# Sums for the first output projection formed inside the loop, in the memory of the finished chunks

## The chip, the cores and the metric

The kernel runs on one core of one Trainium2 chip. The metric is the device time of one execution in microseconds (us). TensorE is called PE, VectorE DVE, ScalarE ACT, GpSimd POOL, and SyncE (which only issues transfers here) SP.

## The reference

Two layers work on `x` of shape (2, 512, 32, 32) in fp32. Layer 0 is attention with sampled keys: for each of 2 images and 8 groups, 64 sample positions are predicted, keys and values are gathered there, and a small network (2 to 128 to 128 to 1) turns every pair of a query position (1024) and a sample position (64) into a bias. After the softmax, the part that matters here follows:

```
out = einsum('bhij,bhjd->bhid', attn, vh)           # heads
out = einsum('bchw,oc->bohw', out, out_w) + out_b   # first output projection
x = x + out
h1 = gelu(einsum('bchw,oc->bohw', bn(x), mlp_w1) + mlp_b1)
x = x + einsum('bchw,oc->bohw', h1, mlp_w2) + mlp_b2
```

Layer 1 is a single-head attention over the 1024 positions of each image with residual.

## The kernel before, in words

**Loop.** Most of the time is a loop of 256 iterations, `for s in range(NS)`, 16 for each of 16 groups (an image `b`, a pair of heads `k`, a half `f`). An iteration evaluates the bias network for four sample positions: `st_layer1` (line 548, DVE) writes `h1` (128x4096), two iterations ahead, in three buffers; `st_layer2` (line 565, PE) multiplies it in 64 recorded matmuls; ACT moves the results out of PSUM into `rx`, `ua`, `ub` (lines 571 and 573); `st_sum` (line 581, DVE) adds them in pairs; POOL issues a transfer that adds `ub` into `ua` (line 583); `st_layer3` (line 604, PE) reduces pairs of iterations into logits, once in two iterations. Beside the loop run two generators, a step per iteration: `bg`, which samples keys and values for the later groups in five chains (`chain`, `sample`), and `tail`, which is the softmax of the group before (`softmax_steps`) and writes the attention weights over the queries in `qa[:, b, k, :]`. The values, already multiplied with the output weights, lie in `vp`.

**First output projection.** After the loop, `project(b, ...)` multiplies `vp` by `qa` for each image as a 2x2 block product in seven products in place of eight. In the order of the code the products are 1, 2, 5, 6, 7, 3, 4; they are called p1, p2, p5, p6, p7, p3, p4 below, and p1' to p4' for image 1. Each is 8 recorded matmuls of 128x512 at line 796. The method needs sums of blocks first: `fold` forms three sums of weight blocks and overwrites a fourth (four adds of 128x512, line 714, on POOL), `spread` does the same for the blocks of `qa` (four adds of 128x1024, lines 717, 718, 719 and 721, on DVE). p1 and p2 read only untouched blocks; p5, p6, p3 and p4 read sums. Image 0 has its sums in a tile `op0`, image 1 in `op1` and `op2`.

**What stands on DVE and PE after the loop.** Each product leaves PE in one of three PSUM buffers of the pool `zp`, and DVE empties it into `xs` or into a temporary (lines 730 and 804), so a product can only start when the one three places before it has been emptied. The softmax of the last group is still to be done then: PE turns its logits (`pt`, line 629), DVE takes the maximum (lines 636 and 637), ACT does the exponentials (642), DVE the reciprocal (647), ACT the scaling (651), PE turns the result back (`pb`, line 660), ACT copies it into `qa` (663), and image 1's `spread` needs it. These steps are queued on DVE among the sums and the emptying of products. The order on each engine is made by a scheduler at build time; each engine then works its own list in order.

**Loads.** SP loads `xs` in sixteen transfers once the loop's buffers below it are free, then the weights of the following MLP in units (`load_unit`: a `w1t` and a `w2t` tile, each with a `fold` on POOL). The MLP's matmuls are at line 850.

Of the kernel before, what the change touches and what calls it, by code (L numbers as in the profile page):

```python
# [8 lines left out]
F32 = mybir.dt.float32  # L9
AF = mybir.ActivationFunctionType  # L10
ALU = mybir.AluOpType
# [3 lines left out]
P = 128  # L15
B, C, H, W = 2, 512, 32, 32
HW = H * W
NCH = C // P
# [8 lines left out]
CHAINS = [[(0, 0)], [(0, 1)], [(0, 2), (0, 3)], [(1, 0), (1, 1)], [(1, 2), (1, 3)]]  # L27
# [21 lines left out]
def conv_seq_kernel(ctx: ExitStack, tc: tile.TileContext, x, xt, kst, cst, vec, wsm, outw, w1, w2, wl, out):  # L49
    nc = tc.nc  # L50
# [28 lines left out]
    qa = cp.tile([P, B, NCH, HW], F32, tag="big", name="qa")  # L79
# [4 lines left out]
    vp = f_pool.tile([P, NCH * B, C], F32, tag="vp", name="vp")  # L84
    sx = f_pool.tile([P, 8, 2, J], F32, tag="sx", name="sx")

    zpp, simpp = (tc.tile_pool(name=n, bufs=c, space=PSUM) for n, c in (("zp", 3), ("simp", 2)))
    zp, simp = zpp.__enter__(), simpp.__enter__()

# [1 line left out]
        return zp.tile([P, 2, 512], F32, tag="ps2", name=name).rearrange("p h n -> p (h n)")  # L91

    groups = [(b, k, f) for b in range(B) for k in range(NCH) for f in range(2)]
    with tc.tile_pool(name="lp", bufs=2) as lp, tc.tile_pool(name="ph", bufs=1) as ph:


        def wake(src, n):
# [575 lines left out]
        for s in range(NS):  # L673
            if s > 0:
                st_sum(s - 1, 2)
            if s % 4 == 0 and s // 4 + 1 < 4 * NG:
                load_tables(s // 4 + 1)
            if s + 2 < NS:
                st_layer1(s + 2)
            st_layer2(s)  # L680


            if s % 4 == 0 and s // 4 + 1 < 4 * NG:
                with tc.issue_after(evicted[s][0]):
                    st_tables(s // 4 + 1)
            st_sum(s, 0)
            with tc.issue_after(evicted[s][1]):
                next(bg, None)
            if tail is not None:
                with tc.issue_after(evicted[s][s % 4 == 0]):  # L690
                    tail = tail if next(tail, 0) is None else None
            if s % 2 == 1 and s >= 3:
                st_layer3(s - 3)
                if (s - 2) % NSL == NSL - 1:
                    tail = softmax_steps(s // NSL - 1)
# [1 line left out]
        st_layer3(NS - 2)  # L697
        tail = softmax_steps(NG - 1)
        next(tail)

    PARTS = {1: (0, 0), 2: (1, 2), 3: (6, 3), 4: (2, 6), 5: (4, 4), 6: (5, 5), 7: (3, 1)}  # L710

    def fold(engine, w, sign=ALU.add):
        for o, u, v, op in ((4, 3, 2, sign), (5, 4, 0, ALU.add), (6, 5, 1, sign), (3, 3, 0, ALU.add)):
            engine.tensor_tensor(w[o], w[u], w[v], op)  # L714

    def spread(x, last=True):
        nc.vector.tensor_tensor(x[4], x[0], x[1], ALU.subtract)
        nc.vector.scalar_tensor_tensor(x[5], x[4], -1.0, x[3], ALU.mult, ALU.subtract)
        nc.vector.tensor_tensor(x[1], x[3], x[1], ALU.subtract)
        if last:  # L720
            nc.vector.scalar_tensor_tensor(x[6], x[5], -1.0, x[2], ALU.mult, ALU.subtract)

    def multiply(pool, order, product, took):
        for p in order:
            ps = pool.tile([P, 2, 512], F32, tag="ps2", name="sw")
            product(ps, *PARTS[p])
            took[p](ps)

    def plus(out, a, b_, op=ALU.add):
        nc.vector.tensor_tensor(out, a, b_, op)  # L730


    def load_g(g, i):
# [25 lines left out]
        nc.vector.scalar_tensor_tensor(t4, t2, -1.0, q[2], ALU.mult, ALU.subtract)  # L759
        return [q[0], t3, q[2], q[3], t1, t2, t4]  # L760

    with tc.tile_pool(name="mp", bufs=1) as mp:
        halves = [(b, h) for b in range(B) for h in range(2)]
        units = [(b, p) for b in range(B) for p in range(NU)]
        wts, accs = {}, {}
# [1 line left out]
        def load_unit(b, p):  # L767
            ws_ = []
            for i, w in enumerate((w1, w2)):
                wt = mp.tile([P, 7, 2, 256], F32, tag=f"w{i + 1}t", name=f"w{i + 1}t", bufs=2)  # L770
                nc.sync.dma_start(out=wt[:, 0:4], in_=w[:, p])
                fold(nc.gpsimd, [wt[:, j] for j in range(7)])
                ws_.append(wt)
            wts[b, p] = ws_
# [6 lines left out]
                load_unit(*units[0])  # L781


        def project(b, parts, wsum, between=lambda: None):
            v, q = vp[:, b * NCH : b * NCH + NCH, :], qa[:, b]
            w = [v[:, k : k + 2, n : n + 256] for k, n in ((0, 0), (2, 0), (2, 256), (0, 256))]
            w += [wsum[:, j] for j in range(3)]
            fold(nc.gpsimd, w)
            x = [q[:, k : k + 2, n : n + 512] for k in (0, 2) for n in (0, 512)] + [parts[:, j] for j in range(3)]
            x11, x12, x21, x22 = quarters(b)  # L790
            t = parts[:, 3]

            def go(ps, a, b_):
                for m in range(2):
                    for k in range(2):
                        nc.tensor.matmul(  # L796
                            ps[:, m, :], w[a][:, k, m * P : (m + 1) * P], x[b_][:, k, :],
                            start=(k == 0), stop=(k == 1),
                        )


            def first(dst, o, u, op):
                for m in range(2):
                    nc.vector.scalar_tensor_tensor(
                        dst[:, m, :], dst[:, m, :], col("outb", o + m), u[:, m, :], ALU.add, op
                    )

            def o1(ps):
                nc.scalar.copy(t, ps)
                first(x11, 0, ps, ALU.add)  # L810

            def o5(ps):
                plus(x22, x22, ps, ALU.subtract)
                plus(x12, x12, ps)

            def o6(ps):
                plus(t, t, ps)
                first(x12, 0, t, ALU.add)

            def o7(ps):  # L820
                plus(t, t, ps)
                first(x22, 2, t, ALU.subtract)
                first(x21, 2, t, ALU.subtract)

            spread(x)
            took = {
                1: o1, 2: lambda ps: plus(x11, x11, ps), 5: o5, 6: o6, 7: o7,
                3: lambda ps: plus(x12, x12, ps), 4: lambda ps: plus(x21, x21, ps, ALU.subtract),
            }
            for p in (1, 2, 5, 6, 7, 3, 4):  # L830
                multiply(zp, (p,), go, took)
                between()


        def normalise(b):
            xb = mp.tile([P, 7, 2, 512], F32, tag="xb", name="xb")
            for j, (o2, h) in enumerate(((0, 0), (0, 1), (1, 0), (1, 1))):
                for m in range(2):
                    o = 2 * o2 + m
                    nc.scalar.activation(  # L840
                        xb[:, j, m, :], xs[:, o, b, h * 512 : (h + 1) * 512], AF.Identity,
                        bias=col("bn2b", o), scale=bns[:, 4 + o : 5 + o],
                    )
            return xb

        def product(w, x):
            def go(ps, a, b_):
                for m in range(2):
                    for k in range(2):
                        nc.tensor.matmul(  # L850
                            ps[:, m, :], w[:, a, k, m * P : (m + 1) * P], x[:, b_, k, :],
                            start=(k == 0), stop=(k == 1),
                        )
            return go
# [34 lines left out]
        def layer2(b, p, w, hm):  # L889
# [31 lines left out]
            plus(v[3], v[3], p5, ALU.subtract)  # L921


        op0 = mp.tile([P, 7, 2, 512], F32, tag="xb", name="op0")
        project(0, op0, op0[:, 4:6].rearrange("p a k n -> p (a k n)")[:, 0:1536].rearrange(
            "p (a k n) -> p a k n", k=2, n=256
        ), lambda: [next(tail, None) for _ in range(3)])
        for _ in tail:
            pass
        xb = normalise(0)  # L930
        op1 = mp.tile([P, 4, 2, 512], F32, tag="acc", name="op1")
        project(1, op1, mp.tile([P, 3, 2, 256], F32, tag="w2t", name="op2", bufs=2))
        spread([xb[:, j] for j in range(7)])
        load_unit(*units[1])
        for pl in (simpp, zpp):
# [22 lines left out]
    with tc.tile_pool(name="sp", bufs=1) as sp:  # L958
# [3 lines left out]
        for b in range(B):  # L962
# [75 lines left out]
            def turn(u, e):  # L1038
                for i in range(2):
                    for m in range(2):  # L1040
                        ps = mq.tile([P, 2, 512], F32, tag="ps2", name="psx")
                        for c in range(8):
                            nc.tensor.transpose(
                                ps[:, c // 4, c % 4 * P : (c % 4 + 1) * P], e[i][:, m, c * P : (c + 1) * P], ident
                            )
                        n = 256 * u + m * P
                        nc.scalar.copy(  # L1047
                            aT[:, i : i + 3 : 2, :, n : n + P],
                            ps.rearrange("p a (c n) -> p a c n", n=P),
                        )  # L1050
                n = slice(256 * u, 256 * u + 256)
                spread([aT[:, j, :, n] for j in range(6)], last=False)

            e0 = scores(0)
            e1 = scores(1)
# [184 lines left out]
```

## Time and profile before

| | us |
|---|---|
| median of 4 runs (2739.53 to 2742.7) | 2741.31 |
| profiled execution, its own time | 2742.95 |
| span of the profile of that execution | 2741.2 |
| PE busy | 2718.9 (99%) |
| DVE busy | 2246.9 (82%) |
| ACT busy | 1686.7 (62%) |
| POOL busy | 374.1 (14%) |
| end of the last loop matmul group, start of p1 | 1988.6 |
| start of the first MLP matmul (line 850) | 2048.36 |

Times in the text are from the start of the span. The profile gives, for each engine, its instructions in order of time, and in brackets how long the engine stood idle before one and what released it. An entry with a count merges several instructions; matmul ends are modelled, so the distance between starts is the better measure on PE.

### The profile page before, as it was taken

Reading aid. Unit: us, or ns where it says so; the run is one execution under the profiler, and the core shown is the slowest. Engines: PE = TensorE matmul, PEld = TensorE weight load, DVE = VectorE, ACT = ScalarE, POOL = GpSimd, SP = SyncE. Lnnn points to the kernel's source line nnn. Section 1 sums busy time; section 2 is a strip of 40 time slices with the busy share of each in tenths; the row PEclk is TensorE's granted clock in tenths of the full one; section 3 lists DMA queues with packets and bytes.
Section 4 is the critical chain, followed back from the end, with each engine's and each line's share of the span. In section 5 each row is a group of like instructions: output and inputs, shape, how many; then the busy total and the mean of one; then the engine's idle time right before and its main releaser. Section 6 shows DMA issues by size and latency. Waiting matters only on the chain.

```text
span 2741.2 us, 46612 instructions
## 1 busy us (share of the span) xinstructions
PE 2718.9 (99%) x20114; PEld 993.8 (36%) x20114; DVE 2246.9 (82%) x1327; ACT 1686.7 (62%) x2164; POOL 374.1 (14%) x430
## 2 busy tenths in 40 slices
PE   9999999999999999999999999999999999999999
PEld 3322323233434323333333333333344444446455
DVE  6999999998999999999999999999774574466454
ACT  4786897788878788876866776686622022124040
POOL 3111111111111111111111111111162232000000
PEclk9999999999999999999999999999999999999999
DMA  5444444444444444444444444444331011000000
GB/s 184 93 95 91 93 99 86 94 101 95 84 91 99 98 85 85 97 90 86 91 94 86 85 95 89 88 93 86 70 138 44 34 46 46 16 16 0 31 0 31
DMA packets 64685, 214.32 MB, mean 78 GB/s; under 512 B 11104, under 2 KB 13664, under 8 KB 61792
## 3 DMA queue, kind: packets, MB, share of 16 engines
q0 software_dynamic: 36864, 135.28, 26.7%
q1 hardware_dynamic: 26752, 74.98, 7.8%
q8 instruction: 159, 2.61, 0.4%
q10 hardware_dynamic: 864, 1.07, 0.1%
q14 instruction: 46, 0.38, 0.0%
HBM read 71.59 MB, written 6.55 MB: 29 GB/s over the span
## 4 chain that ended last, share of the span: by engine, by line
PE 95%; ACT 2%; DVE 1%; issue 1%; DMA 1%; SPq 0%; DVEq 0%; ACTq 0%
PE ps L565 62%; PE sw L850 14%; PE sw L967 9%; PE sim L604 4%; PE sw L1065 2%; PE sw L796 1%; PE psg L454 1%; PE sim L595 1%; DMA fb<-fdr 0%; ACT rx L571 0%; PE pkv L380 0%; PE pt L629 0%; PE pb L660 0%; ACT prod L245 0%; DVE acc L237 0%
## 5 line engine op out<-in xcount | busy, mean ns | idle before, releaser
L565 PE MATMUL ps<-h,cw 128*32 128x512 f32 x16384 | 1789.6, 592 | 7.9 <-ACT rx L571 4.9
L548 DVE CUSTOM_DVE_ANT_1 h<-ta,tb 128x4096 f32<-128x4096 f32 (+1 forms) x257 | 1131.7, 4404 | 87.1 <-PE ps L565 83.4
L565 PEld LDWEIGHTS ps<-h,cw 128*32 128x32 f32 x16384 | 553.2, 110 | 1205.4 <-issue 1149.1
L571 ACT ACTIVATE rx<-ps,sc 128x1024 f32<-128x1024 f32 x512 | 568.9, 1111 | 219.3 <-PE ps L565 215.1
L583 POOL DMA_DIRECT2D ua<-ub x254 | 220.4, 868 | 1696.1 <-DVE ub L581 1608.2
L573 ACT ACTIVATE ua<-ps,sc 128x1024 f32<-128x1024 f32 x256 | 308.4, 1205 | 117.0 <-PE ps L565 116.8
L573 ACT ACTIVATE ub<-ps,sc 128x1024 f32<-128x1024 f32 x256 | 308.0, 1203 | 88.5 <-PE ps L565 88.2
L581 DVE SCALAR_TENSOR_TENSOR ua<-rx,sc,ua 128x1024 f32<-128x1024 f32 x256 | 327.3, 1278 | 34.7 <-ACT ua L573 34.7
L581 DVE SCALAR_TENSOR_TENSOR ub<-rx,sc,ub 128x1024 f32<-128x1024 f32 x256 | 326.6, 1276 | 5.8 <-ACT ub L573 5.6
L850 PE MATMUL sw<-xb,w1t 128*128 128x512 f32 x448 | 193.7, 592 | 1.3 <-DVE xs L730 1.3
L850 PE MATMUL sw<-hm,w2t 128*128 128x512 f32 x448 | 193.6, 592 | 0.0
L730 DVE TENSOR_TENSOR hm<-hm,sw 128x1024 f32<-128x1024 f32 x56 | 67.6, 1220 | 112.5 <-PE sw L850 112.3
L604 PE MATMUL sim<-ua,w3s 128*32 128x512 f32 x1024 | 135.4, 594 | 0.0
L850 PEld LDWEIGHTS sw<-xb,w1t 128*128 128x128 f32 x448 | 85.0, 190 | 108.8 <-issue 105.7
L850 PEld LDWEIGHTS sw<-hm,w2t 128*128 128x128 f32 x448 | 85.1, 190 | 107.1 <-issue 106.4
L859 ACT ACTIVATE hm<-hm,vs 128x512 f32<-128x512 f32 x64 | 42.7, 714 | 129.5 <-DVE hm L730 129.5
L730 DVE TENSOR_TENSOR xs<-xs,sw 128x1024 f32<-128x1024 f32 (+1 forms) x48 | 55.5, 1170 | 75.7 <-PE sw L967 36.0
L529 ACT ACTIVATE ta<-fb,vs 128x512 f32<-128x512 f32 x64 | 88.6, 1384 | 18.2 <-DMA fb<-fdr 18.2
L967 PE MATMUL sw<-aT,vt 128*128 128x512 f32 x224 | 96.7, 593 | 0.3 <-ACT aT L1047 0.3
L884 ACT COPY hm<-sw 128x1024 f32<-128x1024 f32 x8 | 8.1, 1009 | 133.5 <-PE sw L850 133.5
L714 POOL TENSOR_TENSOR w1t<-w1t 128x512 f32<-128x512 f32 x32 | 59.8, 1887 | 112.0 <-DMA w1t<-in_w 111.3
L245 ACT ACTIVATE prod<-qa,vs 128x56 f32<-128x56 f32 (+4 forms) x180 | 64.2, 440 | 0.0
(221 smaller groups left out, 1551.1 us busy)
## 6 DMA issues: line engine op xcount, KB each, us to landing
ua<-ub POOLq DMA_DIRECT2D x254, 512.0 KB, 4.7
fb<-fdr SPq DMA_DIRECT2D x64, 512.0 KB, 5.2
w1t<-in_w SPq DMA_DIRECT2D x8, 1024.0 KB, 5.0
w2t<-in_w SPq DMA_DIRECT2D x8, 1024.0 KB, 5.0
xn<-in_x SPq DMA_DIRECT2D x8, 512.0 KB, 5.3
xnt<-in_xt SPq DMA_DIRECT2D x8, 512.0 KB, 5.9
xs<-in_x SPq DMA_DIRECT2D x16, 256.0 KB, 6.1
out<-xs SPq DMA_DIRECT2D x16, 256.0 KB, 2.1
```

What stands on the lines that cost most here:

```text
L245: nc.scalar.activation(dst, src, AF.Copy, scale=col("dww", 12 * m + t))
L529: nc.scalar.activation(ta.rearrange("p j x -> p x j"), fb[:, 0], AF.Identity, bias=col("cb1"), scale=col("w1x"))
L548: nc.vector._custom_dve(TENSOR_ADD_SAT, out=h1[:, y : y + step].rearrange("p y t x -> p (y t x)"), in0=a.unsqueeze(1).to_broadcast([P, ste ...
L565: nc.tensor.matmul(ps[32 * q : 32 * q + 32, h, :], cw2[:, 32 * z : 32 * z + 32], h1[:, 16 * h : 16 * h + 16, q, :], start=True, stop=True,)
L571: nc.scalar.activation(o, ps, AF.Relu, bias=sc[:, 4 + z : 5 + z])
L573: nc.scalar.activation(o, ps, AF.Relu, bias=sc[:, 4 + z : 5 + z], scale=sc[:, z : z + 1])
L581: nc.vector.scalar_tensor_tensor(r[1], r[0], sc[:, z : z + 1], r[1], ALU.mult, ALU.add)
L583: nc.gpsimd.dma_start(out=sums[s][1], in_=sums[s][3], accum_op=ALU.add)
L604: nc.tensor.matmul(sims[gi][q : q + 32, :], w3s[:, 28 - 4 * i : 60 - 4 * i], sums[s + e][z][:, h, :], start=(i == 0), stop=(i == NSL // 2 ...
L730: nc.vector.tensor_tensor(out, a, b_, op)
L850: nc.tensor.matmul(ps[:, m, :], w[:, a, k, m * P : (m + 1) * P], x[:, b_, k, :], start=(k == 0), stop=(k == 1),)
L967: nc.tensor.matmul(ps[:, m, :], w[:, a, k, c + m * P : c + (m + 1) * P], x[b_][:, k, :], start=(k == 0), stop=(k == nk - 1),)
```

## The change

The temporaries of the chains (pool `ph`) are put at the other end of the memory (`side="right"`). As soon as the last chain has ended, inside the loop, that pool is closed and a pool `op` is opened in its place, with tiles for image 0's sums. The eight adds of image 0's projection are issued from the loop, one per four iterations in the code, and all on DVE. `project` no longer forms sums; image 1's come from `fold` on POOL and `spread` on DVE after the loop, as before, but into buffers that are otherwise the second `w1t` and `w2t`. The MLP's activations get a pool opened after the projection of image 0. In the built program, DVE's list has the eight adds within iterations' work that is about 100 iterations ahead of the loop's end; the order of the two loads of the second MLP unit is reversed, and both stand behind the projection of image 1.

```diff
-    with tc.tile_pool(name="lp", bufs=2) as lp, tc.tile_pool(name="ph", bufs=1) as ph:
+    php = tc.tile_pool(name="ph", bufs=1, side="right")
+    ph = php.__enter__()
+    with tc.tile_pool(name="lp", bufs=2) as lp:
...
+            if bg is not None and state.get(len(CHAINS) - 1, 0) is None:
+                bg = None
+                php.__exit__(None, None, None)
+                opp = tc.tile_pool(name="op", bufs=1, side="right")
+                op = opp.__enter__()
+                op0 = op_blocks(
+                    0, op.tile([P, 3, 2, 512], F32, name="op0x"), op.tile([P, 3, 2, 256], F32, name="op0w")
+                )
+                opt = op.tile([P, 2, 512], F32, name="opt")
+                ready = s
+            if bg is None and s > ready and (s - ready) % 4 == 0 and (s - ready) // 4 <= 8:
+                i = (s - ready) // 4 - 1
+                if i < 4:
+                    spread(op0[1], (i,))
+                else:
+                    fold(nc.vector, op0[0], which=(i - 4,))
...
-                wt = mp.tile([P, 7, 2, 256], F32, tag=f"w{i + 1}t", name=f"w{i + 1}t", bufs=2)
+                wt = wp.tile([P, 7, 2, 256], F32, name=f"w{i + 1}t")
...
-        def project(b, parts, wsum, between=lambda: None):
+        def project(b, w, x, t, between=lambda: None):
-            fold(nc.gpsimd, w)
-            spread(x)
...
-        op0 = mp.tile([P, 7, 2, 512], F32, tag="xb", name="op0")
-        project(0, op0, ...)
+        op1w = wp.tile([P, 5, 2, 256], F32, tag="w2t", name="op1w")
+        op1 = op_blocks(1, wp.tile([P, 3, 2, 512], F32, tag="w1t", name="op1x"), op1w)
+        fold(nc.gpsimd, op1[0])
+        project(0, op0[0], op0[1], opt, lambda: [next(tail, None) for _ in range(3)])
         for _ in tail:
             pass
+        opp.__exit__(None, None, None)
+        mp = top.enter_context(tc.tile_pool(name="mp", bufs=1, side="right"))
         xb = normalise(0)
-        op1 = mp.tile([P, 4, 2, 512], F32, tag="acc", name="op1")
-        project(1, op1, mp.tile([P, 3, 2, 256], F32, tag="w2t", name="op2", bufs=2))
+        spread(op1[1])
+        project(1, *op1, op1w[:, 3:5].rearrange("p a k n -> p a (k n)"))
```

The new function `op_blocks(b, parts, wsum)` only names the blocks: four views of `vp` and three of `wsum`, four views of `qa` and three of `parts`. `fold` and `spread` now take a list of which of their four adds to issue.

## The prediction

> **What bounds the kernel now.** First the page: busy time by engine, and the chain that ended last by engine.
>
> ```profile
> PE 2718.9 (99%) x20114; PEld 993.8 (36%) x20114; DVE 2246.9 (82%) x1327; ACT 1686.7 (62%) x2164; POOL 374.1 (14%) x430
> ...
> PE 95%; ACT 2%; DVE 1%; issue 1%; DMA 1%; SPq 0%; DVEq 0%; ACTq 0%
> ```
>
> PE is the bound nearly everywhere, so the change can win only where PE waits. PE's own timeline shows few such places; the two large ones are just after the loop:
>
> ```profile
> 1999.46 3.60 PE L796 MATMUL sw<-op 128*128 128x512 f32 x8
> 2005.00 0.33 PE L660 MATMUL pb<-kp,sx 128*128 128x128 f32 x1 [1.94 <-ACT sx L651]
> ...
> 2011.29 3.60 PE L796 MATMUL sw<-qa,op 128*128 128x512 f32 x8
> ...
> 2018.16 3.60 PE L796 MATMUL sw<-qa,vp 128*128 128x512 f32 x8
> 2024.48 5.40 PE L796 MATMUL sw<-qa,vp 128*128 128x512 f32 x8 [2.73 <-DVE xs L730]
> 2029.72 7.03 PE L796 MATMUL sw<-op,op 128*128 128x512 f32 x16
> ...
> 2048.36 1.98 PE L850 MATMUL sw<-xb,w1t 128*128 128x512 f32 x4 [1.31 <-DVE xs L730]
> ```
>
> A product takes 3.43 from start to start (2014.73 to 2018.16). **Stall 1:** p6 ends at 1999.46 + 3.43 = 2002.89 and p3 starts at 2011.29: 8.40 us for p7 (3.43) and eight transposes `pb` (1.0: the eight `pt` at 1301.72 to 1302.74). Lost: 4.0. **Stall 2:** p1' ends at 2021.59 and p5' starts at 2029.72: 8.13 for p2' (3.43). Lost: 4.7. Busy time hides part of this, so I asked for the granted clock in stretches (columns: stretch, length, busy time and count of PE, weight loads, DVE, ACT, POOL, then clock, DMA share, GB/s):
>
> ```profile
> 2002.90:2008.60 5.70, 3.61 (x11) 2.12 (x11) 5.03 (x5) 3.45 (x18) 5.62 (x5) 0.71 1.07 404
> ...
> 2024.50:2029.70 5.20, 5.20 (x8) 2.20 (x9) 2.78 (x3) 5.20 (x8) 0.00 (x0) 0.67 0.00 0
> ```
>
> After each wait the clock is low: (1 - 0.67) x 5.20 = 1.7 us lost, in the other (1 - 0.71) x 5.70 = 1.65.
>
> What is late? DVE's timeline:
>
> ```profile
> 1991.03 2.29 DVE L718 SCALAR_TENSOR_TENSOR op<-op,qa 128x1024 f32<-128x1024 f32 x1
> ...
> 1995.45 2.28 DVE L721 SCALAR_TENSOR_TENSOR op<-op,qa 128x1024 f32<-128x1024 f32 x1
> 1997.77 1.41 DVE L804 SCALAR_TENSOR_TENSOR xs<-xs,vs,sw 128x512 f32<-128x512 f32 x2
> 1999.09 0.68 DVE L636 TENSOR_REDUCE mx<-sx 128x8 f32<-128x512 f32 x1
> ...
> 2012.06 2.28 DVE L719 TENSOR_TENSOR qa<-qa 128x1024 f32<-128x1024 f32 x1
> ...
> 2016.53 6.76 DVE L804 SCALAR_TENSOR_TENSOR xs<-xs,vs,op 128x512 f32<-128x512 f32 x4
> 2023.22 2.34 DVE L730 TENSOR_TENSOR xs<-xs,sw 128x1024 f32<-128x1024 f32 x2
> ```
>
> ACT had `sx` ready for the maximum at 1993.9 (copy at 1993.31, 0.59 long), but DVE reached it at 1999.09, behind image 0's sums. The softmax chain (exponentials 2001.56, scaling 2004.60, `pb` 2005.00) is late by that: stall 1. Then `qa` is late (copied 2008.92), image 1's sums are late, and the four adds of line 804 take 6.76 where the same four at 2041.47 take 2.74; p2' waits for the emptying at 2023.22: stall 2.
>
> [...] here waits of 2.1 and 2.73 us drew a slow window; 1.31 at 2048.36 did not. [...] line 717's add takes 1.22 with POOL between its adds and 718 takes 2.29 beside them; POOL's add takes 2.25 there and 1.27 alone.
>
> **The change, part by part.**
>
> *Removed after the loop.* DVE: image 0's four sums (1988.7 to 1997.7 together with the first of image 1; 9.0 us, doubled by POOL). POOL: four of eight weight adds (1989.99 to 1998.82). PE itself waited only 0.5 us for such a sum.
>
> *New order, worked forward.* p1 is done at 1992.1; ACT copies it (1992.40, 1.01), and DVE's first two adds into `xs` can follow at 1993.45: their loads were issued by 1989.2 and took 3.1 to 3.2 us, so 1992.4. They take 1.41, the maximum 0.68, image 1's first sum (now behind it) 1.22, the negation 0.25 (0.17 to 0.66): 1996.9. POOL's four adds for image 1, alone at 1.27, are over at 1995.0 and it then waits for `w1t`, which landed 8.0 after 1992.72, at 2000.7. Exponentials 2.8, reciprocal 0.2, scaling 2.0: 2002.0. That is before p6 ends at 2002.9, so `pb` does not wait: **stall 1, 4.0, goes.** `pb` to 2003.9, p7 to 2007.3, p3 to 2010.8, p4 to 2014.2, p1' to 2017.6.
>
> DVE from there: emptying p6 2003.0 to 2004.2; two adds 3.0 beside POOL's folds, 2007.2; image 1's second and third sums 2.2 and 2.25 (`qa` is ready at 2005.1), 2011.6; emptying p7 1.2, last sum 1.2, 2014.0. POOL has eight adds left from 2000.7; its twelve before took 2003.85 to 2024.43, 1.72 each, so it ends near 2014.5. The four adds of line 804 then run mostly alone: 2.8 to 3.5, 2017.2, and p3 is emptied by 2018.4. p2' could start at 2017.6: a wait near 0.7, less than the 1.31 that drew no slow clock. **Of stall 2's 4.7, about 4.0 goes.** Late next is the emptying of p4' ahead of line 850; that 1.31 stays.
>
> *Added in the loop.* At the end of the last chain (`pkk` at 1227) DVE gets the eight adds spread unevenly over six iterations: 3.1 us in the first (two of 1.22, one of 0.68, overlaps off), then 1.2, 1.2, 1.3, 0.6. The 1.22 is from line 372's 128x1024 add; 0.68 for 128x512 is the nearest row, 678 ns at line 730. The loop there:
>
> ```profile
> 1235.76 4.42 DVE L548 CUSTOM_DVE_ANT_1 h<-ta,tb 128x4096 f32<-128x4096 f32 x1 [0.91 <-PE ps L565]
> 1240.11 1.28 DVE L581 SCALAR_TENSOR_TENSOR ub<-rx,sc,ub 128x1024 f32<-128x1024 f32 x1
> 1241.30 1.28 DVE L581 SCALAR_TENSOR_TENSOR ua<-rx,sc,ua 128x1024 f32<-128x1024 f32 x1
> 1242.63 4.42 DVE L548 CUSTOM_DVE_ANT_1 h<-ta,tb 128x4096 f32<-128x4096 f32 x1
> ```
>
> DVE works 6.73 per iteration of 7.30 (1235.76 to 1250.36 is two): 0.57 spare, and 1.3 spare in the first. Adding instruction by instruction, `h1` starts 0.5 late, then 1.5, 1.7, 2.7, 2.3, and falls back to none within five more iterations. Who waits behind it: `h1` is needed 14.6 after its start and takes 4.4, so 10 us to spare; `rx` buffers, about 3.5 plus 2.3 of PSUM; the transfer of `ub` into `ua`, issued at 1263.14 and 4.5 long, is read by PE at 1271.56: 3.9 to spare, against 2.7 late. I count the loop at nothing; the cover is these spares, and the cost beyond them is the excess itself. From below, 0; from above, see the second rival. Line 317's 1.74 us and its neighbours made DVE similarly late at 490 to 506 and PE ran on.
>
> *Moved.* SP issues the second unit's `w2t` after the last adds of image 1 and its `w1t` behind that, at about 2040 and not 2003.98; then come the four `gg` loads (2047.08 before). Landing takes 5.0 to 8.0, POOL folds both by 2056 and `gg` after them. PE needs that unit one unit later, 48.4 us (2 x 24.2) after 2040: 2088. Cost 0, and if the cover were gone it would be what exceeds 32 us. POOL's folds at 2044 to 2060 fall on DVE adds that read PSUM, which took 1.22 beside POOL's at 2055.60 too. Closing and opening pools adds only waits for things long finished.
>
> **Sum.** 4.0 + 4.0 = 8.0 saved of the profiled span of 2741.2: span 2733.2, own time 2734.9 (1.75 around the span). That execution stands 1.6 above the median of 2741.31, to which I apply the saving: **2733.3**. Own range of this case: 2732.5 (all 8.7) to 2734.8.
>
> **The rivals.**
> 1. *Stall 2 stays.* For it: POOL still has eight adds beside DVE's sums. If all take 2.25, POOL ends at 2018.7, DVE's four adds at 2019.7 and p3's emptying at 2020.9: PE waits 3.3 and draws a slow window of 1.7, so 8.7 - 5.0 = 3.7 saved, 2737.6. Against: DVE has instructions with a PSUM input in between.
> 2. *The loop becomes bound by DVE*, the slower side. If each of the eight sums ran at the doubled length seen beside POOL, DVE would get 14.5 us; less six spares of 0.57 the lateness is 11, over the 3.9 that the `ub` transfer leaves by 7; PE waiting in pieces above 2 us draws two or three slow windows, 3.4 to 5.1. That is 10.5 to 12.2 against 8.0 saved: 2743.8 to 2745.5, with the sums after the loop as forecast; up to 2749 if stall 2 stays as well. It decides once lateness passes 3.9 us by about 5. Against: line 372's add takes 1.22 in the loop, POOL only issuing transfers.
> 3. *It does nothing for PE*: the sums were never what PE waited for (0.5 us), and another step holds the softmax. Saved 0 to 1: 2740.8. Against: DVE's order, the maximum 5.2 us behind its input.
>
> **How the numbers follow.** About 0.2% (5.5 us, so below 2735.8) is what a measurement of this kernel can tell from no change. Main case 0.74; rival 1 0.11; rival 3 0.06; rival 2 0.09, of which 0.05 ends above 2746.8 (lateness past the estimate, or stall 2 staying as well) and 0.04 within the 5.5 us. A little of rival 1, 0.01, ends faster by more than that. So faster 0.75, within 0.20, slower 0.05. The range takes the main case, the unknown of a fully hidden emptying below, and rival 1 above: 2731.8 to 2737.9.
>
> **What would show it.** Right: the maximum at line 681 near 1995 after the loop, no wait before `pb`, no slow clock window after 1990, first line 875 matmul near 2040.4, and gapless PE from 1230 to 1300. Wrong: PE idle at `ps` with DVE or a transfer as releaser between 1230 and 1300 (rival 2), or a wait of over 2 us before p2' (rival 1).

## The result, and the profile after

Median of the kernel after: 2737.06 us (42 runs), of before, run beside it, 2741.12 us (60 runs). The ratio is 0.9985, with a 95% interval of 0.998 to 0.9989: 4.1 us faster, 0.15%. That is half of the 8.0 us forecast, and inside the 0.2% that the prediction took as no change. One of the 42 runs, at 5651.43 us and a granted clock of 0.917, was in a slow state, and the ratio leaves it out. The profiled execution of after has a span of 2736.4 us and an own time of 2738.16.

On the page of the kernel after the busy times have hardly moved. In the chain that ended last PE has 91% where it had 95%, and DVE 4% where it had 1%:

```profile
PE 2718.4 (99%) x20114; PEld 985.0 (36%) x20114; DVE 2244.1 (82%) x1331; ACT 1687.0 (62%) x2164; POOL 362.5 (13%) x426
...
PE 91%; DVE 4%; issue 2%; ACT 2%; DMA 1%; SPq 0%; POOL 0%; DVEq 0%; ACTq 0%; POOLq 0%
```

PE's timeline after the loop (products are at line 822 now, the MLP at 875; in brackets the idle time before a row and its releaser):

```profile
1997.69 7.03 PE L822 MATMUL sw<-op0x,op0w 128*128 128x512 f32 x16
2004.56 1.04 PE L705 MATMUL pb<-kp,sx 128*128 128x128 f32 x8
2005.43 3.60 PE L822 MATMUL sw<-qa,vp 128*128 128x512 f32 x8
...
2015.73 3.60 PE L822 MATMUL sw<-qa,vp 128*128 128x512 f32 x8
2020.94 3.70 PE L822 MATMUL sw<-qa,vp 128*128 128x512 f32 x8 [1.61 <-DVE xs L121]
2024.48 3.60 PE L822 MATMUL sw<-op1x,op1w 128*128 128x512 f32 x8
2028.31 3.67 PE L822 MATMUL sw<-op1x,op1w 128*128 128x512 f32 x8 [0.23 <-DVE xs L830]
```

`pb` follows p6 without a wait: stall 1 is gone. p2' still waits, p6' waits a little where it did not in the first profile of before. The granted clock in two stretches at the same places (the figure after POOL's count):

```profile
2002.90:2008.60 5.70, 5.70 (x21) 3.02 (x20) 4.59 (x4) 1.59 (x4) 5.17 (x4) 1.00 1.02 387
2020.90:2026.10 5.20, 5.16 (x12) 2.39 (x13) 2.83 (x3) 5.20 (x8) 0.00 (x0) 1.00 0.00 0
```

No slow window here. DVE's timeline:

```profile
1995.12 1.41 DVE L830 SCALAR_TENSOR_TENSOR xs<-xs,vs,sw 128x512 f32<-128x512 f32 x2 [5.88 <-DMA xs<-in_x]
1996.44 0.68 DVE L681 TENSOR_REDUCE mx<-sx 128x8 f32<-128x512 f32 x1
...
2009.34 2.29 DVE L112 SCALAR_TENSOR_TENSOR op1x<-op1x,qa 128x1024 f32<-128x1024 f32 x1
2011.55 2.28 DVE L109 TENSOR_TENSOR qa<-qa 128x1024 f32<-128x1024 f32 x1
...
2016.02 3.73 DVE L830 SCALAR_TENSOR_TENSOR xs<-xs,vs,opt 128x512 f32<-128x512 f32 x4
```

The maximum starts 6.16 us after p1 (1990.28), against 10.47 before; DVE now idles 5.88 us ahead of it. Image 1's second and third sums are still twice their length.

**Two distances** carry the comparison below. The *stage* runs from the start of p1 to the first matmul of the MLP. The *loop stretch* runs from the first `sim` row after the last chain (1227.76 in the first profile of before) to p1. It is 760.86 us in before and 761.30 in after. From the first MLP matmul on both kernels take 692.8 us. In the table, the median and the ratio are of a kernel's runs, the ratio against the runs of before that stood beside them; the last three columns are of one profiled execution each.

| run | median, us | ratio to before (95%) | loop stretch | stage | slow windows in the stage |
|---|---|---|---|---|---|
| before, first profile | 2741.12 | | 760.86 | 59.74 | 2 |
| e0: before again | 2742.18 | 1.0006 (0.9998 to 1.0014) | 760.86 | 57.30 | 0 |
| after | 2737.06 | 0.9985 (0.998 to 0.9989) | 761.30 | 53.32 | 0 |
| a3: activation sums alone in the loop | 2736.68 | 0.9985 (0.9978 to 0.9991) | 760.86 | 53.10 | 0 |
| b2: weight sums alone in the loop | 2736.56 | 0.9984 (0.9978 to 0.9991) | 760.86 | 53.03 | 0 |
| c1: after, POOL's MLP adds later | 2735.16 | 0.9977 (0.9968 to 0.9986) | 761.31 | 50.96 | 0 |
| g1: before, POOL behind image 0's sums | 2740.42 | 0.9998 (0.999 to 1.0006) | 760.86 | 57.97 | 2 |
| s2: before, POOL's MLP adds later | 2737.62 | 0.9988 (0.998 to 0.9997) | 760.86 | 55.07 | 1 |
| g2: before, both | 2734.76 | 0.9976 (0.9967 to 0.9985) | 760.86 | 51.38 | 0 |
| f2: c1 with the loop's sums paced | 2734.48 | 0.9975 (0.9966 to 0.9985) | 760.85 | 50.96 | 0 |
| h1: b2 with POOL's MLP adds later | 2735.41 | 0.9977 (0.9968 to 0.9986) | 760.85 | 50.96 | 0 |
| e1: after, sums in the loop doubled | 2738.28 | 0.9989 (0.9981 to 0.9998) | 762.72 | 52.94 | 0 |

The medians alone carry little. The 13 runs of e0 and the 54 runs of the same kernel beside them have medians of 2742.18 and 2740.83, 1.35 us apart. A gap of that size between two rows is therefore no proof, and the readings below rest on the stage and the loop stretch as well.

### The profile page after: what moved, and what is told of

Read it like the earlier page. It is cut to its first block, busy times and chain, and to the rows that moved or that the text cites. A ratio compares the mean times of both kernels' runs of the same rounds, so it can differ in the third digit from the quotient of the medians.

```text
span 2736.4 us, 46606 instructions
## 1 busy us (share of the span) xinstructions
PE 2718.4 (99%) x20114; PEld 985.0 (36%) x20114; DVE 2244.1 (82%) x1331; ACT 1687.0 (62%) x2164; POOL 362.5 (13%) x426
## 4 chain that ended last, share of the span: by engine, by line
PE 91%; DVE 4%; issue 2%; ACT 2%; DMA 1%; SPq 0%; POOL 0%; DVEq 0%; ACTq 0%; POOLq 0%
PE ps L610 58%; PE sw L875 14%; PE sw L994 9%; PE sim L649 4%; PE sw L1092 2%; DVE h L593 2%; PE sw L822 1%; PE psg L499 1%; DVE ub L626 0%; PE sim L640 0%; DVE ua L626 0%; DMA fb<-fdr 0%; ACT rx L616 0%; PE pkv L425 0%; DMA ua<-ub 0%
## 5 line engine op out<-in xcount | busy, mean ns | idle before, releaser
L610 PEld LDWEIGHTS ps<-h,cw 128*32 128x32 f32 x16384 | 546.0, 110 | 1213.2 <-issue 1146.5
```

Of the source, the lines that this page charges most:

```text
L610: nc.tensor.matmul(ps[32 * q : 32 * q + 32, h, :], cw2[:, 32 * z : 32 * z + 32], h1[:, 16 * h : 16 * h + 16, q, :], start=True, stop=True,)
```

## The experiments

**e0: the kernel before, once more.** No edit.

> The kernel before, unchanged, to see how its executions differ among themselves. Theory A (the profiled execution of before drew one slow clock window more than its usual run, and the forecast took both windows as its rule): most runs list a clock one step above the 0.998 of the profile, runs of 0.998 lie about 1.7 us above runs of 0.999, and a new profile shows one slow window or none between the first product after the loop (p1) and the first matmul of the MLP, with 57.5 to 58 us between them where the first profile had 59.74. Theory B (the loop gives back what the stage after it gains): most runs list 0.998, the new profile shows both windows again and 59.7 us in that stage.

PE's timeline in its profile, p2' and p6' of image 1 and the MLP's first row, and the clock behind the wait for `pb` and behind that for p2':

```profile
2024.44 3.70 PE L796 MATMUL sw<-qa,vp 128*128 128x512 f32 x8 [3.04 <-DVE xs L730]
2027.98 3.60 PE L796 MATMUL sw<-op,op 128*128 128x512 f32 x8
2031.85 3.67 PE L796 MATMUL sw<-op,op 128*128 128x512 f32 x8 [0.28 <-DVE xs L804]
...
2047.13 13.14 PE L850 MATMUL sw<-xb,w1t 128*128 128x512 f32 x30 [1.31 <-DVE xs L730]
```

```profile
2006.20:2011.90 5.70, 5.55 (x19) 2.92 (x20) 5.66 (x4) 2.63 (x8) 5.62 (x5) 1.00 0.84 327
2024.40:2029.60 5.20, 5.16 (x12) 2.39 (x13) 2.78 (x3) 5.20 (x8) 1.22 (x1) 1.00 0.00 0
```

The same waits, 1.93 and 3.04 us, drew no slow window, and the stage took 57.30 us (57.5 to 58 expected), 2.44 less than in the first profile. Each run also lists the mean clock of its core. Of the 112 runs of before that stood beside these experiments, 31 listed 0.998 as the first profile did, 71 listed 0.999 and 10 listed 1.0; of the 54 beside e0 the 0.998 runs have a mean of 2742.03 us and the 0.999 runs 2740.63, 1.4 apart where 1.7 was expected. e0's own 13 runs were 7 to 6, so "most runs" was not met by them alone. Theory A holds in its main point: the two windows of the execution that the forecast was read from are not in every run. How many runs have both is not shown. The listed clock of 0.998 is that of 28% of the runs, but it also takes in windows elsewhere: in e0 one near 515, in the first profile one from 2739.14 on, where PE has no matmul left. Against e0 the change gains 3.98 us in the stage (about 2.5 at stall 1 and 1.4 at stall 2) and loses 0.44 in the loop stretch: 3.5, near the 4.1 of the medians.

**a3 and b2: half of the change each.** a3 leaves only the activation sums in the loop; b2 only the weight sums. The comments in the two diffs are not in the kernels.

```diff
# a3
-                else:
-                    fold(nc.vector, op0[0], which=(i - 4,))
...
+    with tc.issue_after(nc.cur_bb.bb.instructions[-1]):   # behind uc on POOL, after the loop
+        fold(nc.gpsimd, op0[0])
# b2
-                if i < 4:
-                    spread(op0[1], (i,))
-                else:
+                if i >= 4:
...
+        with tc.issue_after(newest(mybir.EngineType.DVE)):   # after the loop
+            spread(op0[1])
```

> The kernel after, with only image 0's four activation sums in the loop; its four weight sums go back to POOL after the loop, as before. Nothing is left out. Theory (the activation sums carry all of the gain, the weight sums in the loop carry none, and the loop pays 0.4 us for DVE's lateness): h is at most about 1.5 us late in the loop, the 0.4 us wait at 1272 goes, stall 1 stays away, POOL is about 5 us later with the weights of the first MLP unit, so that stall 2 keeps its wait of 1.6 us or grows by up to 1.5; time within 1 us of the kernel after. Rival (the loop gives back about 2 us, and half of it is due to the weight sums): p1 starts about 1 us earlier in the profile and the time is 1 us or more below the kernel after.

> The kernel after, with only image 0's four weight sums in the loop; its four activation sums go back to DVE after the loop, ahead of the two adds into xs and the softmax's maximum. Nothing is left out. Theory (stall 1 is DVE's order: activation sums ahead of the maximum): the maximum starts 8.4 to 10.5 us after p1 (6.2 in the kernel after, 10.5 before), the transposes pb wait 1.3 to 3 us, with or without a slow window after: 1.3 to 4 us above the kernel after, 2738.4 to 2741. Rival (stall 1 was made by POOL's weight adds beside DVE, so that without them the sums are fast enough): the maximum at 8 us or earlier, pb waits under 0.8, time within 0.8 us of the kernel after.

Either half gives all of the gain, and without the loop's 0.44 us. In a3 POOL was not late: its eight adds ran alone at 1.26 to 1.28 us but for one of 2.24. p2' waited 0.72 us, less than in after, while the `pb` row took 1.48 us where it takes 0.87 in after. In b2 the theory fell. DVE's timeline after the loop:

```profile
1988.99 1.22 DVE L109 TENSOR_TENSOR op0x<-qa 128x1024 f32<-128x1024 f32 x1
1990.25 1.22 DVE L112 SCALAR_TENSOR_TENSOR op0x<-op0x,qa 128x1024 f32<-128x1024 f32 x1
1991.39 1.22 DVE L109 TENSOR_TENSOR qa<-qa 128x1024 f32<-128x1024 f32 x1
1992.53 2.29 DVE L112 SCALAR_TENSOR_TENSOR op0x<-op0x,qa 128x1024 f32<-128x1024 f32 x1
...
1996.28 0.68 DVE L681 TENSOR_REDUCE mx<-sx 128x8 f32<-128x512 f32 x1
```

All four sums stand ahead of the maximum, as before the change, and it starts 6.16 us after p1 (1990.12), as in after, not 8.4 to 10.5: the sums fit into the 5.88 us for which DVE otherwise waits for p1's results and the `xs` loads. The doubling is not all that differs from before. There image 1's first sum stood ahead of the maximum as well, and the sums started 0.13 us behind p1, released by the last `sim`; in b2 they start 1.13 us ahead of it, in memory that the chains have left, and POOL's adds double only the fourth. What the doubling alone costs is read from g1 below. For stall 1 it is enough that one of the two kinds leaves the place where both run; either will do.

**c1: POOL's adds for the first MLP unit held back**, in the kernel after.

```diff
-                load_unit(*units[0])
+                load_unit(*units[0], sums=False)      # loads, no fold
...
         spread(op1[1])
+        for wt in wts[units[0]]:
+            nc.gpsimd.tensor_copy(wt[:, 4, 0, 0:1], op1[1][6][:, 0, 0:1])
+            fold(nc.gpsimd, [wt[:, j] for j in range(7)])
```

The copy of one column reads DVE's last sum, so POOL waits for it there; it writes into a place that the adds behind it overwrite.

> The kernel after, with POOL's eight adds for the first MLP unit held back until DVE has formed image 1's last sum (a copy of one column from that sum ahead of each weight tile's adds); nothing is left out. Theory (POOL's adds beside DVE's sums are what kept 2 us of stall 2): DVE's second and third sum of image 1 take 1.2 us in the place of 2.3, the four adds of line 830 2.8 in the place of 3.7, the waits before p2' (1.61) and p6' (0.23) fall below 0.2, and the stage from p1 to the first MLP matmul takes 51.5 us in the place of 53.32: about 1.8 below the kernel after, 2735.3. Rival (the emptying of p3 is late because of the softmax chain and the copies into qa, not because of POOL): sums get shorter but p2' still waits 1.2 us or more, stage 52.9 or more, 2736.7. Second rival: the held-back adds end too late for the first MLP matmul, which then waits for POOL: they would start at 24 us after p1 and take 10 to 17, and are needed at 51, so this is not expected.

Measured: image 1's sums 1.22 us each; p1' and p2' are one gapless row of 16 (2014.49, 7.03 us), p5' and p6' another; stage 50.96, 2.36 less than after. The adds of POOL were done at 2024.9, 15 us ahead of the MLP. One expectation failed: the four adds of line 831 (830 in after) took 3.74 us and not 2.8, with POOL's held-back work beside them from 2010.79 on. But they start 21.6 us after p1 where they started 25.7 after it, and no product waits for them. The rest of stall 2 was POOL beside DVE.

**g1, s2 and g2: the order of POOL's adds alone**, in the kernel before, with no sum in the loop.

```diff
# g1, in project(): POOL's adds stand behind DVE's sums of image 0
-            fold(nc.gpsimd, w)
...
             spread(x)
+            if b == 0:
+                nc.gpsimd.tensor_copy(w[4][:, 0, 0:1], x[6][:, 0, 0:1])
+                fold(nc.gpsimd, w)
```

In g1 image 1's `fold` is issued behind that of image 0. s2 has the two edits of c1, with the held-back adds behind image 1's `spread` in `project`. g2 has both.

> The kernel before, nothing moved into the loop and nothing left out; only POOL's eight adds for the two images' weights are held back until DVE has formed image 0's fourth activation sum (a copy of one column ahead of them). Theory (stall 1 is made by POOL's adds running beside DVE's sums, each slowing the other; not by the sums' place in the order): image 0's four sums take 1.2 us each in the place of 2.3, the softmax's maximum starts 6 to 7 us after p1 (10.5 in both profiles of before), pb does not wait, stall 1 is gone. POOL is then later with everything behind, its adds for the first MLP unit run until some 32 us after p1, so the four adds of line 804 keep their doubled 6.8 us and stall 2 grows by about what stall 1 gave: p1 to the first MLP matmul 56.2 us (57.30 in the second profile of before), 2739.9. Rival (what the kernel after gains at stall 1 comes from having the sums formed in the loop): the maximum starts at 9 us or later, pb still waits over 1 us, stage and time as before.

> The kernel before, nothing moved into the loop and nothing left out; POOL's adds for the two images' weights run as before, and only its eight adds for the first MLP unit are held back until image 1's last activation sum. With g1 and g2 it makes a square: neither, the first, the second, both. Theory (two separate places where POOL slows DVE; the wait before pb comes from the first, the wait before p2' from the second, and lateness from the first is carried into the second only as far as DVE has no slack): the wait before pb stays at 1.9 us, image 1's second and third sums take 1.2 us and the four adds of line 804 about 3.7 in the place of 6.76, p2' waits under 0.3 us, p1 to the first MLP matmul 53.4 us without slow windows, 55 with one: 2737.3. Rival (stall 2 is carried over from stall 1): p2' still waits 1.5 us or more, stage 55.5 or more without slow windows, 2739.5.

> The kernel of the run before with, as well, POOL's eight adds for the first MLP unit held back until image 1's last activation sum. Nothing is moved into the loop, nothing left out. Theory (all of the two stalls is POOL against DVE, so an order of POOL's adds alone gives at least what the change gives): no doubled sums, waits before pb, p2' and p6' under 0.3 us, stage 51.0 to 51.5, loop as before, 2734.9: below the kernel after by 2 us. Rival (the weight sums come too late for the product p5, which is due 7.4 us after p1, while the held-back adds give the second sum at 7.4 to 9.4): p5 waits up to 2 us and the stage takes 53, 2736.8. Second rival (the sums formed in the loop are needed): stage 56 or more, 2740.

First the place that g1 changes. POOL's timeline in the first profile of before, its first and its fifth add, the fifth after DVE's sums:

```profile
1989.99 2.25 POOL L714 TENSOR_TENSOR op<-vp 128x512 f32<-128x512 f32 x1
...
1998.82 1.27 POOL L714 TENSOR_TENSOR op<-vp 128x512 f32<-128x512 f32 x1
```

g1, DVE's timeline and then PE's:

```profile
1992.91 1.22 DVE L721 SCALAR_TENSOR_TENSOR op<-op,qa 128x1024 f32<-128x1024 f32 x1
...
1995.48 0.68 DVE L636 TENSOR_REDUCE mx<-sx 128x8 f32<-128x512 f32 x1
...
2013.45 6.76 DVE L808 SCALAR_TENSOR_TENSOR xs<-xs,vs,op 128x512 f32<-128x512 f32 x4
```

```profile
2002.83 0.47 PE L660 MATMUL pb<-kp,sx 128*128 128x128 f32 x2
...
2021.40 6.33 PE L800 MATMUL sw<-qa,vp 128*128 128x512 f32 x8 [3.70 <-DVE xs L730]
```

The sums are short, at before's place and in before's number, and the maximum starts 7.24 us after p1 (a little past the 6 to 7 expected) where it started 10.47 after it: the doubling alone cost 3.2 us there. `pb` has no wait. But POOL's MLP adds now fall on the four adds of line 808, 6.76 us as before, and p2' waits 3.70: stall 1's gain came back as stall 2, with two slow windows in this profile. s2 is the reverse: `pb` waits 1.93, drawing one window, and p2' does not wait, p1' and p2' being one row:

```profile
2004.34 0.33 PE L660 MATMUL pb<-kp,sx 128*128 128x128 f32 x1 [1.93 <-ACT sx L651]
...
2017.53 7.03 PE L797 MATMUL sw<-qa,vp 128*128 128x512 f32 x16
```

With both orders neither stall is left. g2, DVE, POOL and PE:

```profile
1991.93 1.22 DVE L718 SCALAR_TENSOR_TENSOR op<-op,qa 128x1024 f32<-128x1024 f32 x1
...
1995.81 1.27 POOL L714 TENSOR_TENSOR op<-vp 128x512 f32<-128x512 f32 x1
...
2004.11 0.47 PE L660 MATMUL pb<-kp,sx 128*128 128x128 f32 x2
...
2015.39 7.03 PE L801 MATMUL sw<-qa,vp 128*128 128x512 f32 x16
```

g2 is 2.3 us below the kernel after, with the change not made at all; its profile has the loop stretch 0.44 and the stage 1.94 shorter, 2.4 together. The expected times (2739.9, 2737.3, 2734.9) came out at 2740.42, 2737.62 and 2734.76.

**f2 and h1: c1 without the loop's cost.** f2 ties each of the eight sums to the place in DVE's list where its iteration's `st_sum` stands; h1 is b2 with the edit of c1.

```diff
             st_sum(s, 0)
+            pace = nc.cur_bb.bb.instructions[-1]
...
+                with tc.issue_after(pace):
                     if i < 4:
                         spread(op0[1], (i,))
...
```

> The kernel after with POOL's first MLP unit held back behind image 1's last sum, as in the run c1, and with the eight sums in the loop evenly spaced, one to every fourth operation index in DVE's order. Nothing is left out. Theory (the loop pays 0.45 us, the wait of sim at 1272 for the transfer of ub into ua, because DVE gets 3.1 us of sums in one iteration): h at most 1.3 us late, the sim row at 1272 is one row of 8 again, from the first sim after the last chain to the first MLP matmul 811.8 us (812.27 in c1, 814.62 in the kernel after), 2734.7. Rival (the 0.45 us is not from the lateness of DVE): 812.3 and 2735.2.

> The run b2 (only image 0's four weight sums in the loop, its activation sums on DVE after the loop) with POOL's adds for the first MLP unit held back behind image 1's last sum. Nothing is left out. Theory: no wait in the loop as in b2 and no stall 2 as in c1: from the first sim after the last chain to the first MLP matmul 811.8 us, stage 51.0 us, 2734.7. Rival (the activation sums on DVE after the loop make image 1's sums late once more): p2' waits over 1 us, stage 52.5 or more, 2736.3.

From the first `sim` row to the MLP both took 811.81 us (811.8 expected; 814.62 in after). The medians of c1, g2, f2 and h1, 2734.5 to 2735.4, are not told apart by these runs; all are some 2 us below the kernel after.

**e1: the loop's sums doubled.** Each sum is followed by one of its size into a spare buffer.

```diff
                     spread(op0[1], (i,))
+                    nc.vector.tensor_tensor(opt, qa[:, 0, 0:2, 0:512], qa[:, 0, 2:4, 512:1024], ALU.subtract)
                 else:
                     fold(nc.vector, op0[0], which=(i - 4,))
+                    nc.vector.tensor_tensor(opt[:, 0], vp[:, 0, :], vp[:, 1, :], ALU.subtract)
```

> The kernel after with each of the eight sums in the loop followed by a second one of the same size into a buffer that is not read before it is overwritten: 16 sums, 15.2 us more or less where the kernel after has 7.6. They fall over some ten iterations in the place of six, 0.6 to 1.2 us in each where 0.57 is spare. Theory (the loop bears DVE's lateness up to 3.9 us, less where the transfer of ub into ua takes longer than its usual 4.5 us, and what exceeds it is lost by PE one for one): h up to about 6 us late, PE waits at sim in several iterations, together 1.5 to 2.5 us; from the first sim after the last chain to p1 762.5 to 763.5 us where the kernel after has 761.30 and before 760.86; time 1.3 to 2.2 above the kernel after, 2738.8, or 1.7 more if a wait draws a slow window. Rival (the loop pays for a busy DVE in proportion, 0.45 us for eight sums and so 0.9 for sixteen): 761.8, 2737.5. Second rival (PE becomes bound by DVE for good): over 765.

The loop stretch took 762.72 us, 1.86 more than before and inside the theory's 762.5 to 763.5. `h` (the tile of `h1`) was some 5 us late by 1291. PE lost it in pieces, of which those that the trace shows are about 0.4 us long at `sim` (at 1271 and 1333), and none drew a slow window. The time, 2738.28, is 0.5 under the theory's.

## Why the prediction was right in part

The measured time lies inside the stated range of 2731.8 to 2737.9, but 3.8 us above the 2733.3 named and at the end that was set by rival 1 (stall 2 stays, 2737.6). It is there for other reasons than that rival's alone: about half of stall 2 stayed, and more than half of what is missing is in the base. That it fell inside is in part luck. What was given a chance of 0.75, a time below 2735.8, did not come about, and two of the signs named for it failed: the first line 875 matmul came at 2043.60 and not near 2040.4, and the `sim` row of 1272.78 is broken.

**Right.** Stall 1's 4.0 us: p6's end to p3 took 8.40 before and 4.31 after, though 1.6 of the 4.0 was the slow window that came with it (6.83 in e0). The maximum came 6.16 us after p1 (the forecast's 1995 is 6.4 after its p1 of 1988.6), scaling was done 13.2 after (forecast 13.4), the first two adds into `xs` at 4.84 (forecast 4.83). The moved loads cost PE nothing. The 1.31 us ahead of the MLP stayed. DVE's lateness in the loop, worked out as 0.5, 1.5, 1.7, 2.7, 2.3, was 0.46, 1.45, 1.59, 2.66, 2.26.

**Wrong: "of stall 2's 4.7, about 4.0 goes".** Stall 2 went from 4.7 to 1.9 (8.13 to 5.32, less 3.43), and p6' lost 0.4 that the sum did not have: 1.6 us. The terms that were too small: `w1t` reached POOL 13.1 us after p1, not 12.1, so POOL's eight adds ended 27.0 after and not 25.9; the two adds behind p6 took 3.41 and not 3.0, the four of line 830 3.73 where 2.8 to 3.5 were given. p2' then waited 1.78 where the sum had 0.7. c1 shows what most of these small terms have in common: with POOL held back the two adds behind p6 take 1.42 and image 1's second and third sums 1.22 each, so that the four adds of line 830, still 3.74, start 4.1 us earlier after p1. The forecast took stall 2 for a consequence of stall 1 ("then `qa` is late"); s2 shows that it had its own cause, since there stall 1 stands and p2' does not wait.

**Wrong: "I count the loop at nothing".** The lateness was right; the spare was not. It was worked out with a transfer of `ub` into `ua` of 4.5 us. What the trace says of the transfer issued at 1267.01 in after:

```profile
DMA to landing us min/median/max: 6.1/6.1/6.1
```

In e0 the same transfer took 4.5. 2.7 late and 1.6 longer is 4.3, over the 3.9 to spare by 0.4. The trace of before had such landings: its 254 transfers of this kind took 4.5 to 8.0 us, with a median of 4.7. Why this one grew was not tested, but the trace of after gives a hint. Nearly all of it has moved 4.1 us after its issue, as in e0, but the rest goes on at some 13 GB/s, where the transfer had moved 202, until shortly before it lands. A packet of the queue that the profile lists as "instruction" starts at 1270.39, in the midst of the transfer's data; in e0 it starts at 1268.80, behind them. So the lateness seems to have brought the transfer and that packet together. PE's `sim` row shows the wait, broken in two:

```profile
1272.78 1.44 PE L649 MATMUL sim<-ua,w3s 128*32 128x512 f32 x6
1273.66 0.60 PE L649 MATMUL sim<-ua,w3s 128*32 128x512 f32 x2
```

It runs 0.44 past the 1.04 of a whole row, and p1 is 0.44 later. f2, with the lateness spread out, has the 760.85 of before. So rival 2 (the loop bound by DVE) named the right place; its price needed more lateness than there was, and e1 shows the slope beyond it.

**Wrong: the base.** The sum took 3.35 us of slow clock, out of one execution, from a median of runs most of which list a higher clock than that execution's 0.998. In e0 the stage had none, and was 2.44 us shorter; the page's own time of 2742.95, 1.6 above the median, was the hint, and the text used it for the level only and not for the saving. With the three terms, 8.0 - 1.6 - 0.44 - 2.44 = 3.5, the difference of the traces of e0 and after.

**The cause, deeper than the prediction went.** It read that DVE reached the maximum "behind image 0's sums" and took the sums' place for the cause. g1 and g2 show that the sums may stay where they were. In the first profile of before each of image 0's last three sums took 2.28 to 2.29 us with POOL's adds beside them, and POOL's first four adds took 2.13 to 2.25; in g1, where POOL's adds come behind those sums, the same three took 1.22 each and POOL's eight adds 1.26 to 1.28. Run side by side, each was some 0.9 to 1.1 us longer. By what mechanism they slow each other, the runs do not show. The prediction knew of the doubling and booked it as a length of DVE's work, not as a thing that an order of POOL's work could remove.

**What stays open.** The split of medians between windows and waits is from single profiles; how often each of before's two waits draws a window was not counted. And no run moves the second MLP unit's loads alone. In before POOL has four adds for that unit among the emptying of products (2017.69 to 2024.43); in after and in every run made from it they come behind the stage. How much of the 1.4 us at stall 2 is due to that is not shown.

## What to carry to other kernels

Where two engines slow each other, ask first what happens if one of them merely waits: copies of one column as gates gave 2.3 us more here than moving eight sums a hundred iterations ahead. And treat a slow clock window in a profile as one draw: read a saving from a second profile as well before it is taken off a median. A spare that hangs on a transfer is only as good as the longest landing in the trace (8.0 us in before), not the median one (4.7).

## What the runs showed of the hardware

- **A wait's length alone did not tell whether the clock would fall; how much of it lay in one window did in the two traces divided below.** Waits of 1.93 us ahead of `pb` drew a slow window in s2 and none in e0; ahead of p2', 2.73 drew one (first profile of before) and 3.04 did not (e0). The wait for `rx` near 515, 2.27 to 3.05 us in the twelve profiles, drew one in nine of them and none in the first profile of before, in s2 and in e1 (2.47 to 2.57 there). The first profile of before and that of after show a pattern. The record of the granted clock in the trace of before has a clock of 0.50 for 3.413 us from 2005.27 and from 2025.75, and from 2739.14 to its end; in after, for 3.413 us from 514.40, and from 2736.47 to its end. Each of these starts lies a whole number of times 3.4133 us behind the first entry of its record (at 5.06 in before, at 5.81 in after): 586, 592 and 801 times, and 149 and 800. Divided there into windows, before has three of full clock in which PE stood still for 1.94 us or more (1.94, 2.14 and 2.46), and after has two (2.16 and 3.41); a slow one follows each. In all others of full clock PE stood still for 1.79 us or less in before and 1.49 or less in after, and a slow one follows none. Two pairs of neighbours from the first profile of before, then one from e0 (behind each window stand its length and PE's busy time; the granted clock is the figure after POOL's count):

```profile
2001.86:2005.27 3.41, 1.47 (x4) 0.33 (x2) 2.77 (x4) 3.14 (x19) 3.33 (x4) 1.00 1.04 394
2005.27:2008.68 3.41, 3.26 (x10) 2.06 (x10) 3.38 (x3) 1.35 (x6) 3.41 (x3) 0.50 1.07 409
513.65:517.06 3.41, 1.62 (x16) 0.55 (x20) 3.41 (x1) 3.41 (x5) 0.16 (x1) 1.00 0.87 143
517.06:520.47 3.41, 3.41 (x36) 0.94 (x32) 1.62 (x2) 3.38 (x6) 0.87 (x1) 1.00 0.56 175
```

```profile
2019.65:2023.06 3.41, 1.75 (x5) 0.45 (x3) 3.41 (x3) 0.00 (x0) 3.33 (x3) 1.00 0.00 0
2023.06:2026.47 3.41, 2.03 (x5) 1.06 (x6) 2.52 (x4) 3.10 (x5) 2.56 (x2) 1.00 0.00 0
```

In e0 a border at 2023.06 cuts the wait ahead of p2' into 1.66 and 1.38 us, and no slow window followed the longer wait. The prediction's rule, that 1.31 us is safe and 2.1 is not, looked at the length alone. Matmul ends are modelled, so the gap between 1.79 and 1.94 us is no surer than they are. The borders lie elsewhere against the program in these three profiles: the one nearest ahead of p1 stands 0.4 us ahead of it in before, 0.9 in e0 and 1.3 in after. In this sense the cost of a wait of 2 to 3 us was a matter of chance here.

- **Small instructions took longer too.** The negation of the maximum (128x8) took 0.17 us in after and 1.23 in b2, with POOL's add beside it; POOL's 128x2 add `uc` took 0.19 in after and 1.22 in b2, with DVE's sum beside it. The maximum itself took 0.68 everywhere, in b2 too, where a POOL add of 1.26 us ran beside it.
- **One recurring transfer, the same bytes:** 4.5 to 8.0 us to land in before, with a median of 4.7; at one iteration 4.5 in before and in e0, and 6.1 in after and in c1, where it is issued 2.7 us later.
